# A later start for the image's split, scans moved to other steps, and one small product moved to GpSimd, in a four-layer convolution network on one core

## The chip, the cores and the metric

The kernel runs on one core of a Trainium2 chip. A core has TensorE (PE, matrix products), VectorE (DVE), ScalarE (ACT), GpSimd (POOL) and SyncE (SP), which issues most transfers. Each engine works through its own list of instructions in the order in which the program gave them, and waits on semaphores for the others. The metric is device time in microseconds (us), taken as the median of several executions. A separate execution is recorded by the hardware profiler; single durations and waits come from it.

## What is computed

The input `x` has 4 images of 32 x 32 pixels with 16 channels. Four layers follow each other, each `x = x + layer(group_norm(x))`. Layers 0, 1 and 3 are convolutions with a filter for every pixel:

```
first   = einsum('ijyx,byxc->bijc', M, inputs)
shifted = conv(inputs, kern)        # 32*32*16 filters of 3x3x16, one set for each (i, j)
diff    = relu(inputs[:, None, None] - shifted)
second  = einsum('ijyx,bijyxc->bijc', W, diff)
return first - second
```

(The last layer sums over the other pair of pixel indices.) Layer 2 is an interval layer: running maxima and minima over a 32 x 32 triangle, then two steps that take `max_k sigmoid(f[i,k] Wf + r[k,j] Wr + b)` over k, then a sigmoid of a product.

## The kernel before

Numbers of layers in the kernel count the three convolutions as 0, 1 and 2; the interval layer is done ahead of the third one, so "layer 2" in the code is the last convolution with the interval layer before it. The images go in two groups of two. A phase is one convolution layer on one group; there are six phases, in the order (group 0, layer 0), (group 1, layer 0), (group 0, layer 1), and so on. While TensorE does one phase, what the next phase needs is prepared behind it.

A phase has 8 chunks of 128 output pixels (`t`), and a chunk 32 steps: 16 channels `f` times 2 images `b`. So a phase has 256 steps, and the kernel 1536. In a step, TensorE fills one of four pairs of accumulation banks (`pc`) with 14 matmuls that run two at a time: `first_part` does those with WU and WL, then ScalarE scales the pair (L607), then `second_part` does those with WD and W9. Then VectorE reads the pair, takes the smaller of it and zero, multiplies by the weights WT of the chunk and sums up (L623, called junk<-pc). `first_part` of a step is issued before `second_part` of the step before it. At each 32nd step VectorE also adds the sums to X (L637).

float32 values are split into a high part (their upper bits, a bit mask, L176) and the rest[...]. L176 is used on the weights (`upper_w`) and on the image (`upper_x`). "Masking" here is L176, not `mask2`, which is a small constant of the interval layer.

Three streams of other work are laid between the steps, in an order written out by generators. No scheduler moves anything.

- `prep_parts` prepares the weights, one unit (4 channels) in eight steps, two units ahead. The eight parts are: L176 on DVE; W9 on ACT (L152); WD's first half on ACT (L209), and W (L222) and two WL (L224) on POOL; WD's second half, and `prep` of the next unit on POOL (L186); WU (L212) on ACT with WD (L213) on POOL, twice; the load of a later unit's weights on SP (L101); nothing. Each part ends with a `yield` that says whether the step is free for other work ("idle"): true for the first and the last two, false for the rest.
- `behind(phase)` does everything else for the next phase: in layer 2 `interval_layer`, then `before_conv`, then the first terms. What it yields is the number of steps until it is asked again; `IDLE` (0) means the next step that the weights' stream calls idle.
- `conv_layer` runs the steps and asks both.

`before_conv` normalizes the image, writes it to DRAM (L340) and reads it back as shifted copies, 24 transfers into `raw` (L350, on SP). After a last `yield 4`, `split` makes the image's parts for each of the two images: L176 on DVE, iz on POOL (L253), iy on ACT (L257), im on ACT (L152) and later on DVE (L155), iyz on POOL (L260). With layers 0 and 1, and when the second group is prepared, the first-term matmuls (L380) come after it, with their transposes and sums (L387, L390).

`interval_layer` transposes (L463), fills (L471), runs two scans of 512 elements in each direction (`running`, L481), a reordering copy between the directions on POOL (L488) and a triangle select (L492). Then `right_side` (L515, copies L518), `left` (L502, copy L527), and `step` twice, with names a and b: eight sums of 33 x 33 on POOL (L534), each followed six steps later by a maximum on DVE (L541), then a sigmoid (L545) and four transfers (L547). `constants` makes the layer's constants early in phase 0; `mask2` is reduced on DVE (L405), and half of it is negated on DVE (L409).

In the trace a wait of DVE for `raw<-xs` is a wait for the shifted copies.

Of the kernel before, what the change touches and what calls it, by code (L numbers as in the profile page):

```python
# [19 lines left out]
GC = GB * C  # L20
# [21 lines left out]
def net_kernel(ctx: ExitStack, tc: tile.TileContext, x, xq, xi, convs, iv_w, iv_b, out):  # L42
# [21 lines left out]
    nc = tc.nc  # L64
# [23 lines left out]


    IDLE = 0  # L90
    RAWS = 2
    PLAIN = 2
    AHEAD = 2
    FIRST = 3
    raws, units, chunks = {}, {}, {}

    def load_raw(u):
        if u < n_chunks * NU:
            n = u // NU
            raws[u] = wpool.tile([P, 4, FU, P], F32, tag="raw", bufs=RAWS, name=f"raw_{u}")  # L100
            nc.sync.dma_start(raws[u], convs[phases[n // NT][1]][2][n % NT, u % NU])  # L101
# [49 lines left out]
    def halve(dst, src, mask):  # L151
        nc.scalar.activation(dst, src, AF.Copy, scale=mask[:, 1:2])  # L152
# [16 lines left out]
    def image(v, x):  # L169
        return v.rearrange("... (y x) -> ... y x", x=x)[..., :H]  # L170

    def upper(src, name):

        t = work.tile([P, 2, NH], F32, tag="upper", bufs=2, name=f"upper_{name}")
        t = t.rearrange("p s (y x) -> p s y x", x=src.shape[3])
        nc.vector.tensor_scalar(  # L176
            t.bitcast(I32), src.bitcast(I32), HIGH, None, op0=ALU.bitwise_and
        )
        return t.rearrange("p s y x -> p s (y x)")
# [12 lines left out]
    def prep_parts():  # L192

        for u in range(PLAIN, n_chunks * NU):
            units[u] = [
                wpool.tile([P, 2, FU, P], F32R, tag=tag, bufs=AHEAD + 1, name=f"{tag}_{u}")
                for tag in ("WU", "WL", "WD")  # L200
            ] + [wpool.tile([P, FU, P], F32R, tag="W9", bufs=AHEAD + 1, name=f"W9_{u}")]
            src = raws.pop(u)
            w8 = src[:, :2].rearrange("p s f k -> p s (f k)")
            w9 = src[:, 2]
            WU, WL, WD = (t.rearrange("p s f k -> p s (f k)") for t in units[u][:3])
            W9 = units[u][3]

            def scaled(s):
                nc.scalar.activation(WD[:, s], high[:, s], AF.Copy, scale=-EPS)  # L209

            def difference(s):
                nc.scalar.copy(WU[:, s], high[:, s])  # L212
                nc.gpsimd.tensor_tensor(  # L213
                    WD[:, s], WD.bitcast(F32)[:, s], WL.bitcast(F32)[:, s], ALU.add
                )

            high = upper(src[:, :2], f"w{u}")
            yield True
            halve(W9, w9, low_w)
            yield False  # L220
            scaled(0)
            nc.gpsimd.tensor_tensor(W9, W9.bitcast(F32), src[:, 3], ALU.add)  # L222
            for s in range(2):
                nc.gpsimd.tensor_tensor(WL[:, s], w8[:, s], high[:, s], ALU.subtract)  # L224
            yield False
            scaled(1)
            prep(u + 1)
            yield False
            difference(0)
            yield False  # L230
            difference(1)
            yield False
            load_raw(u + RAWS)
            yield True
            yield True

    def prep_plain(u, at=0, to=FU, eng=nc.gpsimd):
        if at == 0:
# [8 lines left out]

    def split(eng, g, b, name, pause=IDLE):

# [24 lines left out]
    def group_norm(g, name, dst, gap):  # L274
# [40 lines left out]
        yield 2  # L315
        yield IDLE
        rstd = work.tile([P, GC // 2], F32, tag="rstd", name=f"rstd_{name}")
# [10 lines left out]
    def before_conv(g, layer):  # L328
        xn = work.tile([P, NT, GC], F32, tag="xn", bufs=2, name=f"xn_{g}_{layer}")
        xns[g] = xn  # L330
        yield from group_norm(g, f"c{g}{layer}", xn, 1 if layer == 2 else 4)

        nc.vector.transpose(  # L335
            xt[g][:, :, 1 : 1 + H], xn
        )
        inner = xs[g][:, HP : HP + H * HP].rearrange("p (t r n) -> p r t n", r=ROWS, n=HP)
        for r in range(ROWS):
            nc.sync.dma_start(inner[:, r], xt[g][GC * r : GC * (r + 1)])  # L340
        yield 2
        xsv = xs[g].rearrange("(b c) n -> c b n", b=GB)
        at = 0
        for slot, row, tap in [(2, row, 8) for row in range(4)] + [
            (tap // 4, tap % 4, tap) for tap in range(8)
        ]:
            for h in range(2):
                off = (HI * h + tap // 3) * HP + tap % 3
                r0 = 64 * h + C * row
                nc.sync.dma_start(  # L350
                    raw[r0 : r0 + C, slot, :, :RUN], xsv[:, :, off : off + RUN]
                )
            at += 1
            if at % 3 == 0:
                yield 1
        yield 4
        for b in range(GB):
            yield from split(nc.gpsimd, g, b, f"{g}{layer}")
            yield IDLE
            halve(image(im9[g][:, b], H), image(raw[:, 2, b], HP), low_x)  # L360
            for s in range(2):
                difference(nc.gpsimd, g, b, s)
            yield 3
            halve_rest(image(im9[g][:, b], H), image(raw[:, 2, b], HP), low_x)
            yield 1
# [35 lines left out]
    def constants():  # L401
        nc.scalar.dma_start(wv, iv_w)
        nc.scalar.dma_start(bv, iv_b)
        mask2 = const.tile([P, GB], F32, name="mask2")
        nc.vector.tensor_reduce(  # L405
            mask2, ident.rearrange("p (s b c) -> p b s c", b=GB, c=C), axis=AX.XY, op=ALU.add
        )

        nc.vector.tensor_scalar_mul(mask2[GC : 2 * GC], mask2[GC : 2 * GC], -1.0)  # L409
        yield 2  # L410

        def blocks(dst, k, mask, n, p0=0):
            p = dst.shape[0]
            nc.gpsimd.tensor_tensor(
                dst,
                wv[p0 : p0 + p, k, :].unsqueeze(1).to_broadcast([p, n, C]),
                mask[p0 : p0 + p].unsqueeze(2).to_broadcast([p, n, C]),
                ALU.mult,
            )

        nc.gpsimd.memset(rt, 0.0)
        yield 1


        for k, hidden, name in ((0, None, "f0"), (3, 2, "f1"), (6, 5, "f2")):
            n = 64 if hidden is None else 96
            t = const.tile([n, GB, C], F32, name=name)
            blocks(t[:64], k, mask2, GB)
            if hidden is not None:
                blocks(t[64:], hidden, mask2, GB, 64)  # L430
            iv[name] = t.rearrange("p k c -> p (k c)")
            yield 1
        for k, name in ((1, "r0"), (4, "r1")):
            t = const.tile([64, NQ * GB, C], F32, name=name)
            for q in range(NQ):
                blocks(t[:, q * GB : (q + 1) * GB, :], k, mask2, GB)
            iv[name] = t.rearrange("p k c -> p (k c)")
            yield 1
    def interval_layer(g):
# [4 lines left out]
        n = H * H  # L444
# [19 lines left out]
        yield 2  # L464
        yield IDLE
        nc.scalar.mul(one[GC:], one[:GC], -1.0)
# [10 lines left out]
        def running(dst, src):  # L477

            for half in range(2):
                o = slice(n // 2 * half, n // 2 * (half + 1))  # L480
                nc.vector.tensor_tensor_scan(  # L481
                    dst[:, o], resets[:, o], src[:, o], 0.0, op0=ALU.add, op1=ALU.max
                )
                yield 3


        yield from running(one[:, ::-1], other[:, ::-1])
# [36 lines left out]
        def step(name, ftp, bias):  # L524
# [6 lines left out]
            for i in range(QI + 1):  # L531
# [11 lines left out]
                yield 6  # L543
            yield IDLE
            nc.scalar.activation(s, s, AF.Sigmoid, bias=bias)  # L545
# [98 lines left out]
    def conv_layer(phase, behind):  # L644


        wait, when_idle = 0, False
        accs[phase] = work.tile([P, NT, GC], F32, tag="acc", bufs=2, name=f"acc_{phase}")
        for t in range(NT):
            n = phase * NT + t  # L650
            steps = [(f, b) for f in range(C) for b in range(GB)]
            if n == 0:
                steps.sort(key=lambda s: (s[0] // FU, s[1]))
            for at, (f, b) in enumerate(steps):
                idle = next(parts, True) if n or at >= FIRST else True
                if at == 4:
                    load_chunk(n + 1)
                step = (phase, t, f, b)
                open_steps.append((step, first_part(step)))
                if len(open_steps) > 1:  # L660
                    second_part(*open_steps.pop(0))
                wait -= 1
                if wait <= 0 and (idle or not when_idle):
                    wait = next(behind, 1 << 20)
                    when_idle = wait == IDLE
        for _ in behind:
            pass

# [167 lines left out]
    parts = prep_parts()  # L836
    for phase in range(len(phases)):
        conv_layer(phase, behind(phase))
# [78 lines left out]
```

## Time and profile before

| | |
|---|---|
| median of 3 executions | 2600.67 us (2600.32 to 2601.96) |
| the profiled execution | 2597.44 us, recorded span 2595.7 us |
| mean granted TensorE clock | 0.999 |
| L623, DVE, x1536 | 1878.9 us, 1223 ns each |
| L607, ACT, x1520 | 1531.5 us, 1008 ns each |
| L176 on weights, DVE, x190 | 140.2 us, 738 ns each |
| L481 scan, DVE, x8 | 11.9 us, 1491 ns each |
| L409, DVE, x1 | 3.8 us |
| L541 maxima, DVE, x32 | 41.0 us, 1281 ns each |
| L534 sums, POOL, x32 | 75.8 us, 2367 ns each |
| transfers raw<-xs, x120 | 67.8 KB each, 2.4 us to landing |

How to read it: the page gives the busy time of each engine. The list of waits says which engine stood idle for which other, in total, how often, and the longest. The timeline gives single instructions: start, duration, engine, line, operation, output and inputs, and in brackets the idle time just before and what ended it. The table of windows gives the busy time of each engine in a stretch, and the granted TensorE clock in its column PEclk (1.00 is full speed). A duration on DVE or POOL includes time in which the instruction was already issued and could not go on.

### The profile page before, as it was taken

How to read it: one execution, taken by the hardware profiler on the slowest of the kernel's cores; microseconds unless marked ns; L12 is line 12 of the kernel's file. 1: busy time of each engine (PE TensorE's matmuls, PEld its weight loads, DVE VectorE, ACT ScalarE, POOL GpSimd, SP SyncE). 2: the span in 40 equal slices, each digit the busy share in tenths (PEclk: the TensorE clock that was granted, in tenths of full speed). 3: DMA queues.
4: the chain of work that ended last, by engine and by line, in shares of the span. 5: the costliest groups of instructions: out<-in, count | busy, mean ns of one | idle time of the engine just before them, and what ended most of it. 6: DMA issues, size and time to landing. Idle time of an engine off the chain costs nothing.

```text
span 2595.7 us, 56475 instructions
## 1 busy us (share of the span) xinstructions
PE 2561.7 (99%) x21906; PEld 2048.5 (79%) x21906; DVE 2151.6 (83%) x3652; ACT 2094.7 (81%) x2549; POOL 1564.6 (60%) x1288
## 2 busy tenths in 40 slices
PE   8999999999999999999999999999999999999999
PEld 5887888878888877888887877787777777788887
DVE  8887778888777877777888988889889888777777
ACT  4787888888888877888887888888888888788886
POOL 4656555575555556555566766576767666455553
PEclk9999999999999999999999999999999999999999
DMA  4423222232222432222222222322222234222220
GB/s 152 165 79 114 90 90 92 83 129 88 87 95 90 153 117 76 97 90 90 91 98 90 90 84 86 123 93 90 78 89 97 92 118 155 76 99 90 90 91 19
DMA packets 50285, 254.14 MB, mean 98 GB/s; under 512 B 12129, under 2 KB 14049, under 8 KB 24929
## 3 DMA queue, kind: packets, MB, share of 16 engines
q1 hardware_dynamic: 49056, 249.94, 28.3%
q8 instruction: 172, 2.82, 0.4%
q14 instruction: 97, 0.79, 0.1%
q10 hardware_dynamic: 832, 0.58, 0.1%
q0 software_dynamic: 128, 0.02, 0.0%
HBM read 248.99 MB, written 0.98 MB: 96 GB/s over the span
## 4 chain that ended last, share of the span: by engine, by line
PE 92%; DVE 3%; DMA 2%; issue 2%; SPq 1%; ACT 1%; DVEq 0%; ACTq 0%
PE pc L577 91%; DVE junk L623 2%; SPq L350 1%; PE pf L380 1%; DMA raw<-in_g 1%; DMA raw<-xs 1%; ACT pc L607 0%; DMA xs<-xt 0%; SPq L340 0%; DVE upper_w L176 0%; PE ps_l L502 0%; DMA XQ<-in_xq 0%; DVE s_b L541 0%; PE ps_r L515 0%; DVE xt L335 0%
## 5 line engine op out<-in xcount | busy, mean ns | idle before, releaser
L623 DVE SCALAR_TENSOR_TENSOR junk<-pc,WT 128x1024 f32<-128x1024 f32 x1536 | 1878.9, 1223 | 399.8 <-PE pc L577 355.4
L607 ACT ACTIVATE pc<-pc 128x1024 f32<-128x1024 f32 x1520 | 1531.5, 1008 | 446.9 <-PE pc L577 385.6
L577 PE MATMUL pc<-iy,WU 64*128 64x512 f32 x6080 | 968.7, 394 | 18.5 <-DVE junk L623 18.5
L577 PE MATMUL pc<-iyz,WD 64*128 64x512 f32 x6080 | 965.6, 393 | 3.3 <-ACT pc L607 2.6
L577 PE MATMUL pc<-iz,WL 64*128 64x512 f32 x6080 | 964.3, 393 | 0.0
L222 POOL TENSOR_TENSOR W<-W,raw 128x512 fp32r<-128x512 f32 x190 | 250.7, 1320 | 832.1 <-ACT W L152 829.0
L577 PEld LDWEIGHTS pc<-iy,WU 64*128 64x128 f32 x6080 | 577.0, 185 | 162.4 <-DVE junk L623 27.2
L577 PEld LDWEIGHTS pc<-iyz,WD 64*128 64x128 f32 x6080 | 579.0, 185 | 141.2 <-ACT pc L607 6.6
L577 PEld LDWEIGHTS pc<-iz,WL 64*128 64x128 f32 x6080 | 580.1, 185 | 133.6
L577 PE MATMUL pc<-im,W 64*128 64x512 f32 x3072 | 621.4, 397 | 0.0
L224 POOL TENSOR_TENSOR WL<-raw,upper_w 128x512 fp32r<-128x512 f32 x380 | 487.3, 1305 | 4.4 <-DVE upper_w L176 4.4
L213 POOL TENSOR_TENSOR WD<-WD,WL 128x512 fp32r<-128x512 f32 x380 | 488.5, 1308 | 0.0
L577 PEld LDWEIGHTS pc<-im,W 64*128 64x128 f32 x3072 | 293.4, 185 | 71.1 <-issue 3.6
L209 ACT ACTIVATE WD<-upper_w 128x512 fp32r<-128x512 f32 x380 | 237.1, 624 | 10.9 <-DVE upper_w L176 10.9
L212 ACT CAST WU<-upper_w 128x512 fp32r<-128x512 f32 x380 | 233.5, 615 | 1.3 <-issue 1.3
L186 POOL TENSOR_TENSOR raw<-raw,pick 128x512 f32<-128x512 f32 x190 | 201.2, 1059 | 7.9 <-DMA raw<-in_g 5.3
L176 DVE TENSOR_SCALAR upper_w<-raw 128x1024 int32<-128x1024 int32 x190 | 140.2, 738 | 0.1
L152 ACT ACTIVATE W<-raw,low_w 128x512 fp32r<-128x512 f32 x190 | 135.9, 715 | 0.1
L623 DVE DVE_READ_ACCUMULATOR junk<-pc,WT 128x1 f32 x1536 | 127.3, 83 | 0.0
L534 POOL TENSOR_TENSOR tables<-ft_b,rt 128x1089 f32<-128x1089 f32 x16 | 37.9, 2366 | 5.3 <-ACT ft_b L527 5.3
L534 POOL TENSOR_TENSOR tables<-ft_a,rt 128x1089 f32<-128x1089 f32 x16 | 37.9, 2368 | 0.0
L253 POOL TENSOR_TENSOR iz<-raw,upper_x 128x512 fp32r<-128x512 f32 x20 | 23.8, 1202 | 23.2 <-DVE upper_x L176 23.2
(134 smaller groups left out, 384.2 us busy)
## 6 DMA issues: line engine op xcount, KB each, us to landing
raw<-in_g SPq DMA_DIRECT2D x190, 1024.0 KB, 4.9
WT<-in_w SPq DMA_DIRECT2D x48, 512.0 KB, 3.5
MT<-in_mt SPq DMA_DIRECT2D x6, 2048.0 KB, 12.2
raw<-xs SPq DMA_DIRECT2D x120, 67.8 KB, 2.4
raw<-in_xi SPq DMA_DIRECT2D x3, 271.0 KB, 4.8
raw<-in_xi SPq DMA_DIRECT2D x1, 813.0 KB, 8.1
first<-in_g SPq DMA_DIRECT2D x1, 768.0 KB, 8.6
xs<-xt SPq DMA_DIRECT2D x20, 34.0 KB, 2.1
```

The lines of the kernel that those rows point to most:

```text
L152: nc.scalar.activation(dst, src, AF.Copy, scale=mask[:, 1:2])
L176: nc.vector.tensor_scalar(t.bitcast(I32), src.bitcast(I32), HIGH, None, op0=ALU.bitwise_and)
L186: eng.tensor_tensor(raws[u][:, 1, at:to], raws[u][:, 1, at:to], pick[:, f0 + at : f0 + to].unsqueeze(2).to_broadcast([P, to - at, P]), ALU ...
L209: nc.scalar.activation(WD[:, s], high[:, s], AF.Copy, scale=-EPS)
L212: nc.scalar.copy(WU[:, s], high[:, s])
L213: nc.gpsimd.tensor_tensor(WD[:, s], WD.bitcast(F32)[:, s], WL.bitcast(F32)[:, s], ALU.add)
L222: nc.gpsimd.tensor_tensor(W9, W9.bitcast(F32), src[:, 3], ALU.add)
L224: nc.gpsimd.tensor_tensor(WL[:, s], w8[:, s], high[:, s], ALU.subtract)
L534: nc.gpsimd.tensor_tensor(t, ft[:, i, :].unsqueeze(1).to_broadcast([P, T1, T1]), rt, ALU.add,)
L577: nc.tensor.matmul(ps[:, h, :], lhsT=w[r], rhs=v[r], start=first and k == 0, stop=k == len(pairs) - 1, skip_group_check=not first,)
L607: nc.scalar.activation(ps, ps, AF.Copy, scale=1.0 + EPS)
L623: nc.vector.scalar_tensor_tensor(junk, ps.rearrange("p h n -> p (h n)"), 0.0, chunks[n], op0=ALU.min, op1=ALU.mult, accum_out=accs[phase][ ...
```

## The change

Three things are changed. `before_conv` yields 12 steps (7 in layer 2) in place of 4 between the last transfers of the shifted copies and `split`. In `running`, each scan waits for a step that the weights' stream calls CALM, a new second kind of step: the third, fourth and fifth of its eight parts; after a scan the yield is 1 in place of 3. `conv_layer` is rewritten to know the two kinds; a positive yield and IDLE mean what they meant. The negation in `constants` goes from VectorE to GpSimd.

```diff
+    CALM = -1
...
             high = upper(src[:, :2], f"w{u}")
-            yield True
+            yield (IDLE,)
             halve(W9, w9, low_w)
-            yield False
+            yield ()
             scaled(0)
...
-            yield False
+            yield (CALM,)
             scaled(1)
             prep(u + 1)
-            yield False
+            yield (CALM,)
             difference(0)
-            yield False
+            yield (CALM,)
             difference(1)
-            yield False
+            yield ()
             load_raw(u + RAWS)
-            yield True
-            yield True
+            yield (IDLE,)
+            yield (IDLE,)
...
-        yield 4
+        yield 7 if layer == 2 else 12
         for b in range(GB):
             yield from split(nc.gpsimd, g, b, f"{g}{layer}")
...
-        nc.vector.tensor_scalar_mul(mask2[GC : 2 * GC], mask2[GC : 2 * GC], -1.0)
+        nc.gpsimd.tensor_scalar_mul(mask2[GC : 2 * GC], mask2[GC : 2 * GC], -1.0)
...
                 o = slice(n // 2 * half, n // 2 * (half + 1))
+                yield CALM
                 nc.vector.tensor_tensor_scan(
                     dst[:, o], resets[:, o], src[:, o], 0.0, op0=ALU.add, op1=ALU.max
                 )
-                yield 3
+                yield 1
...
-        wait, when_idle = 0, False
+        kind, wait = 1, 0
...
-                idle = next(parts, True) if n or at >= FIRST else True
+                may = next(parts, (IDLE, CALM)) if n or at >= FIRST else (IDLE, CALM)
...
                 wait -= 1
-                if wait <= 0 and (idle or not when_idle):
-                    wait = next(behind, 1 << 20)
-                    when_idle = wait == IDLE
+                if wait <= 0 and (kind > 0 or kind in may):
+                    kind = wait = next(behind, 1 << 20)
```

## The prediction

> **What bounds the kernel now.** Time is set by TensorE (page, parts 1 and 4):
>
> ```profile
> PE 2561.7 (99%) x21906; PEld 2048.5 (79%) x21906; DVE 2151.6 (83%) x3652; ACT 2094.7 (81%) x2549; POOL 1564.6 (60%) x1288
> ...
> PE 92%; DVE 3%; DMA 2%; issue 2%; SPq 1%; ACT 1%; DVEq 0%; ACTq 0%
> ```
>
> No matmul is changed, so only TensorE's idle time can be won or enlarged. The wait views of PE and of DVE:
>
> ```profile
> PE pc L577 <- DVE junk L623: 18.5, 14, 3.0
> ...
> PE pc L577 <- ACT pc L607: 2.6, 6, 0.6
> ```
>
> ```profile
> DVE junk L623 <- PE pc L577: 355.4, 937, 1.2
> DVE upper_x L176 <- DMA raw<-xs: 19.3, 5, 4.7
> ```
>
> DVE idles 355 us yet holds TensorE up 14 times: bursts. Asking for the PE waits window by window places all 14. Five stalls (2.83, 1.31, 3.01, 2.50, 2.27; sum 11.9) follow the five L176 that wait for the shifted copies. Four (0.84 and 1.48, in each of two interval layers; 4.6) follow the scans. One (0.80) follows L409, and four (0.36, 0.20, 0.33, 0.23; 1.1) lie among step b's maxima.
>
> Rule of the burst: in DVE's timeline L623 starts every 1.63 us when it waits for matmuls and every 1.37 when behind, so DVE catches up 0.27 a step. At 210.44 L623 starts 4.7 late (due 1.63 after 204.09) and TensorE stalls 2.83; so about 2.0 us of lateness are free (four PSUM pairs), and the rest is a stall.
>
> A stall costs more than its gap. The third one in PE's timeline, and the clock after it:
>
> ```profile
> 957.60 1.22 PE L577 MATMUL pc<-iy,WU 64*128 64x512 f32 x4 [3.01 <-DVE junk L623]
> ...
> 960.69 0.63 PE L577 MATMUL pc<-iy,WU 64*128 64x512 f32 x4
> ```
>
> ```profile
> 957.20:960.60 3.40, 3.00 (x14) 2.41 (x16) 3.27 (x7) 2.82 (x4) 3.02 (x3) 0.50 0.19 80
> ```
>
> Seven matmul pairs take 3.09 us where a full-speed step takes 1.63: the clock column says 0.50. The 2.83 stall is followed by the same (213.1 to 216.5); the 2.50 one is not. I price the two half-clock stretches at 3.09 - 1.63, about 1.5 us each. And any stall has 0.26 of restart: at the fourth one the im matmuls start at 1683.09 and, a step later, at 1687.49; 4.40 less the usual 1.63 is 2.76, for a gap of 2.50.
>
> [...]L409 on 32x2 elements ends at 114.21, just when GpSimd's row ends at 114.19; scans take 1.21 beside an idle GpSimd and 1.70 to 1.85 beside L213. [...]here 2.83 and 3.01 cost the clock, 2.50 didn't.
>
> **The change, part by part.**
>
> *Longer wait (yield 4 to 12, to 7 in layer 2).* Counting L623 in the instruction orders of both kernels, L176 on the image moves from steps 112, 304, 560 to 120, 312, 568, and from 992, 1248 to 995, 1251. SP's order is unchanged, so the copies land when they did: 4.5, 3.0, 4.7, 4.0, 3.2 us after DVE came for them. DVE now comes 8 x 1.63 = 13 or 3 x 1.63 = 4.9 us later, so all five are there, with 0.9 us to spare in the fourth, and being under 2.0 late would be free. Removed: 11.9 + 5 x 0.26 + 2 x 1.5 = 16.2. Moved along: iz, iyz on POOL, iy, im on ScalarE, L155, and in layers 0 and 1 the first-term matmuls with L387 and L390. None of these issues a DMA. Eight steps keep the place relative to the weights' preparation (period 8), and where they stood they made DVE at most 1.5 late (L623 at 241.18, its matmuls done at 239.66): under 2.0, so nothing. In layer 2 the first L176 on the image comes one read after a mask and may find POOL at W or WL: 0.1 + 0.1 + 1.3 late at most, free too; the last L155 stays at 1014, ten steps before it is needed. Bounds: gain 16.2; if the two layer-2 transfers are later still by 2 us, 11.
>
> *L409 to GpSimd.* It leaves DVE's queue, where L623 stood behind 3.81 us:
>
> ```profile
> 110.40 3.81 DVE L409 TENSOR_SCALAR mask<-mask 32x2 f32<-32x2 f32 x1
> ```
>
> On POOL it stands between the two L213 of one unit; the nearest row, L306 TENSOR_SCALAR on POOL, is 254 ns. Behind it wait WD and the small L414, and the unit's matmuls come eight steps later: hidden. Removed: 0.80 + 0.26 = 1.1. The 0.72 stall just before comes from ScalarE's late L607 behind the issue of L403 and stays. Bounds 0 to 1.3.
>
> *Scans.* Before (DVE, then POOL):
>
> ```profile
> 1365.55 1.85 DVE L481 TENSOR_TENSOR_SCAN tables<-tables 64x512 f32<-64x512 f32 x1
> ...
> 1373.43 1.68 DVE L176 TENSOR_SCALAR upper_w<-raw 128x1024 int32<-128x1024 int32 x1
> ...
> 1387.11 1.21 DVE L481 TENSOR_TENSOR_SCAN tables<-tables 64x512 f32<-64x512 f32 x1
> 1388.24 1.71 DVE L176 TENSOR_SCALAR upper_w<-raw 128x1024 int32<-128x1024 int32 x1
> ```
>
> ```profile
> 1365.00 3.49 POOL L213 TENSOR_TENSOR WD<-WD,WL 128x512 fp32r<-128x512 f32 x2
> 1372.45 2.10 POOL L488 COPY tables<-tables 64x1024 f32<-64x1024 f32 x1 [3.95 <-DVE tables L481]
> ```
>
> Line 1373.43 is a mask behind L488, which the second scan released; lines 1387.11 and 1388.24 are scan and mask on end. The four scans now precede L623 number 807, 813, 821, 823 (were 806, 809, 815, 818); masks stay at 802, 810, 818, 826. So at least three reads (L623) lie between a scan and the next mask, but all four stand where POOL works. A scan delays L623 by 0.93 alone (1370.02 to 1372.31, less 1.37) and 1.57 locked (1364.40 to 1367.33). By the 0.27 rule lateness goes: 0.3 before 807, about 1.5 after; 0.8 before 813, 1.1 to 2.0 after; under 0.5 before 821, 0.8 to 1.1 after; 0.55 to 0.85 at 822, and the scan at 823 probably stands behind L213: 2.3. That is a stall of 0.3 + 0.26 per layer, 1.1 in both. Removed: 2 x (0.84 + 1.48 + 2 x 0.26) = 5.7. Net 4.6; bounds 0 (every scan waits out a whole L213 of 1.3) and 5.7.
>
> *What moves with them.* L488, L492, the right-side matmuls L515 with their copies L518, L502, L527 and L534 go along by one to five steps; PE does the same matmuls, and L492 (1.26 on POOL) has five steps before L515 needs it. Step a's maxima L541 move from 837 ... 879 to 840 ... 882. L545 with its four DMAs on SP waits for an idle slot and stays, and so does step b at 904 ... 946. Modulo 32, step a now lies exactly as step b does, and step b is where the last four stalls are. At a multiple of 32, L637 comes just ahead of a maximum:
>
> ```profile
> 1572.35 1.50 DVE L637 SCALAR_TENSOR_TENSOR X<-acc,X 128x32 f32<-128x32 f32 x1
> 1573.77 1.28 DVE L541 TENSOR_REDUCE s_b<-tables 128x33 f32<-128x1089 f32 x1
> ```
>
> L637 waits there for L534 on POOL (1571.42 to 1573.80), and POOL's order around it is the same in both steps now. So step a takes over step b's cost: 0.36 + 0.20 + 2 x 0.26 = 1.1 per layer. Added: 2.2; bounds 0 and 3.
>
> *Sum.* 16.2 + 1.1 + 4.6 - 2.2 = 19.7 us against the profiled span of 2595.7. That execution took 2597.44, so it lies 3.2 below the median; the stalls are fixed by the program, so I subtract from the median: 2600.67 - 19.7 = 2581.0.
>
> **Rivals.** (1) The scans win nothing, as the lock meets each of them, and step a pays: 16.2 + 1.1 - 2.2 = 15.1, or 2585.6; with step a at 3 each and the tight layer-2 waits half paid, 2588. For it: POOL is busy at all four places. Against: no mask follows close. (2) Step a doesn't inherit the stalls and the scans are free: 23.0, or 2577.7. Against: equal orders. (3) The copies aren't what it says: the landing moves along with the wait, and only scans and mask gain: 3.5, or 2597.2. Against: SP issues the copies back to back for 11 us whatever DVE does. (4) Slower: POOL becomes the bound between the scans and the end of step a (806 to 882, ten units of 8 steps in each interval layer). Each lock holds POOL up, WD comes late, and TensorE waits for it. A unit lasts 8 x 1.63 = 13.1 us; POOL's work in it is 7.4 (L222, two L224, L186, two L213) and 8/6 of an L534 of 2.37: 10.6. The room is 2.5 us a unit, and weights are ready some six steps, 10 us, ahead, another 1.0 over ten units. So it decides from 3.5 us of lock a unit, and eats up the gains from 4.5 (19.7 over twenty units is 1.0). At 5 us: 2 x (10 x 2.5 - 10) = 30, or 2611. Against: the locked unit seen here lost 1.0 (L213 3.49 for 2.54), and PE waited for POOL 0.7 us in all.
>
> **How the numbers follow.** Forecast 0.64 (2578 to 2584), (1) 0.22, (2) 0.07, (3) 0.04, (4) 0.03. Measurement tells about 0.2%, 5.2 us, from no change: faster means under 2595.5. Forecast, (1) and (2) are all faster, and so is a part of the range between (1) and (3): 0.94; same 0.035; slower 0.025. Range 2577.5 to 2588: it takes in (2) and (1).
>
> **What would show it.** Right: no DVE wait for raw<-xs (before 19.3 us), no clock of 0.50 between start and end; L409 gone from DVE, about 0.25 us on POOL; PE's wait for L623 down from 18.5 to 3 or 4 us; new stalls near 1465 in step a; at most small ones at the scans. Wrong: waits for raw<-xs left in layer 2, stalls over 1 us at the fourth scan, or PE waiting for WD.

## The result, and the profile after

The changed kernel takes 2578.74 us (median of 4 executions, 2578.01 to 2578.97); the kernel before, beside it, 2600.49 (2597.4 to 2601.96). The ratio is 0.9917, with a 95% interval of 0.9900 to 0.9935: 21.7 us less, faster by 0.8%. The profiled spans are 2576.3 and 2595.7 us, 19.4 apart. In the line numbers of the changed kernel, L176 has become L177, L409 L410, L481 L483, L534 L536, L541 L543, L577 L579, L607 L609, L623 L625 and L637 L639.

The page of the changed kernel, parts 1 and 4:

```profile
PE 2558.4 (99%) x21906; PEld 2058.9 (80%) x21906; DVE 2150.0 (83%) x3651; ACT 2094.3 (81%) x2549; POOL 1565.7 (61%) x1289
...
PE 97%; DVE 2%; issue 1%; ACT 0%; DMA 0%; DVEq 0%; ACTq 0%
```

PE's share of the chain of waits has gone from 92% to 97%, and the transfers (2%) have left it. Its waits, and those of DVE:

```profile
PE pc L579 <- ACT pc L609: 3.0, 7, 0.6
PE pc L579 <- DVE junk L625: 2.3, 8, 0.4
```

```profile
DVE junk L625 <- PE pc L579: 351.3, 928, 1.2
...
DVE junk L625 <- DMA raw<-xs: 0.2, 1, 0.2
```

TensorE's wait for the reading of the sums is down from 18.5 us to 2.3. What is left is eight stalls of about 0.36 and 0.20, four of them in the two steps a and four in the two steps b. None of the five masks of the image waits for the shifted copies any more, where DVE waited 19.3 us before: the 0.2 us left under that name stand before an L625, not before a mask.

The first mask of the image, in DVE's timeline, now follows its L625 at once, where it stood 4.50 us before:

```profile
214.90 1.22 DVE L625 SCALAR_TENSOR_TENSOR junk<-pc,WT 128x1024 f32<-128x1024 f32 x1 [0.40 <-PE pc L579]
216.05 0.69 DVE L177 TENSOR_SCALAR upper_x<-raw 128x1024 int32<-128x1024 int32 x1
216.66 1.22 DVE L625 SCALAR_TENSOR_TENSOR junk<-pc,WT 128x1024 f32<-128x1024 f32 x1
```

Two of the scans, and the mask after them:

```profile
1364.46 2.03 DVE L483 TENSOR_TENSOR_SCAN tables<-tables 64x512 f32<-64x512 f32 x1
...
1381.18 2.02 DVE L483 TENSOR_TENSOR_SCAN tables<-tables 64x512 f32<-64x512 f32 x1
...
1386.97 0.69 DVE L177 TENSOR_SCALAR upper_w<-raw 128x1024 int32<-128x1024 int32 x1
```

The scans have become longer (1.72, 2.03, 1.30 and 2.02 us in this layer; 1.85, 1.21, 1.70 and 1.21 before), since they stand where GpSimd works. This longer time beside the other engine is what "lock" stands for in the prediction and in one expectation below: in the kernel before a scan took 1.21 beside an idle GpSimd and 1.85 beside L213 (at 1365.55), and the two L213 took 3.49 there where two took 2.54 elsewhere (at 1379.71). How the two engines hold each other up was not shown. But the mask after them is 0.69 long and three L625 away, and between 1340 and 1400 us the list names no wait of PE.

The negation on GpSimd:

```profile
111.24 0.22 POOL L410 TENSOR_SCALAR mask<-mask 32x2 f32<-32x2 f32 x1
```

3.81 us on DVE have become 0.22 on GpSimd. And step a, in DVE's timeline, where the kernel before had no stall:

```profile
1450.40 1.51 DVE L639 SCALAR_TENSOR_TENSOR X<-acc,X 128x32 f32<-128x32 f32 x1
1451.83 1.28 DVE L543 TENSOR_REDUCE s_a<-tables 128x33 f32<-128x1089 f32 x1
...
1455.53 1.31 DVE L177 TENSOR_SCALAR upper_w<-raw 128x1024 int32<-128x1024 int32 x1
```

It is the picture of step b from the prediction, almost to the hundredth: L639 held for 1.51, a maximum right behind it, then a mask held for 1.31.

### The profile page after: what moved, and what is told of

It is laid out like the page before. It is cut to its first block, busy times and chain, and to the rows that moved or that the text cites. A ratio compares the mean times of both kernels' runs of the same rounds, so it can differ in the third digit from the quotient of the medians.

```text
span 2576.3 us, 56475 instructions
## 1 busy us (share of the span) xinstructions
PE 2558.4 (99%) x21906; PEld 2058.9 (80%) x21906; DVE 2150.0 (83%) x3651; ACT 2094.3 (81%) x2549; POOL 1565.7 (61%) x1289
## 4 chain that ended last, share of the span: by engine, by line
PE 97%; DVE 2%; issue 1%; ACT 0%; DMA 0%; DVEq 0%; ACTq 0%
PE pc L579 96%; DVE junk L625 1%; PE pf L381 1%; ACT pc L609 0%; PE ps_l L504 0%; DMA XQ<-in_xq 0%; DVE s_a L543 0%; DVE s_b L543 0%; PE ps_r L517 0%; DVE X L639 0%; ACT L547 0%; ACT L319 0%; ACT s_a L547 0%; PE ps_y L565 0%; DVE raw L786 0%
## 5 line engine op out<-in xcount | busy, mean ns | idle before, releaser
L625 DVE SCALAR_TENSOR_TENSOR junk<-pc,WT 128x1024 f32<-128x1024 f32 x1536 | 1879.2, 1223 | 401.3 <-PE pc L579 351.3
L609 ACT ACTIVATE pc<-pc 128x1024 f32<-128x1024 f32 x1520 | 1531.6, 1008 | 445.6 <-PE pc L579 383.9
L579 PE MATMUL pc<-iy,WU 64*128 64x512 f32 x6080 | 967.5, 394 | 2.7 <-DVE junk L625 2.3
L579 PE MATMUL pc<-iyz,WD 64*128 64x512 f32 x6080 | 965.6, 393 | 3.0 <-ACT pc L609 3.0
L579 PE MATMUL pc<-iz,WL 64*128 64x512 f32 x6080 | 964.0, 392 | 0.0
L579 PEld LDWEIGHTS pc<-iy,WU 64*128 64x128 f32 x6080 | 579.7, 185 | 141.6 <-DVE junk L625 9.9
L579 PEld LDWEIGHTS pc<-iyz,WD 64*128 64x128 f32 x6080 | 580.9, 185 | 138.5 <-ACT pc L609 8.6
L579 PEld LDWEIGHTS pc<-iz,WL 64*128 64x128 f32 x6080 | 582.4, 185 | 129.7
L579 PE MATMUL pc<-im,W 64*128 64x512 f32 x3072 | 621.8, 397 | 0.0
L214 POOL TENSOR_TENSOR WD<-WD,WL 128x512 fp32r<-128x512 f32 x380 | 488.4, 1309 | 0.1
L579 PEld LDWEIGHTS pc<-im,W 64*128 64x128 f32 x3072 | 294.5, 185 | 69.2 <-issue 3.4
L213 ACT CAST WU<-upper_w 128x512 fp32r<-128x512 f32 x380 | 233.7, 615 | 0.9 <-issue 0.9
L177 DVE TENSOR_SCALAR upper_w<-raw 128x1024 int32<-128x1024 int32 x190 | 136.6, 719 | 0.1
L625 DVE DVE_READ_ACCUMULATOR junk<-pc,WT 128x1 f32 x1536 | 127.7, 83 | 0.0
L536 POOL TENSOR_TENSOR tables<-ft_b,rt 128x1089 f32<-128x1089 f32 x16 | 38.0, 2373 | 5.3 <-ACT ft_b L529 5.3
L536 POOL TENSOR_TENSOR tables<-ft_a,rt 128x1089 f32<-128x1089 f32 x16 | 37.9, 2366 | 4.6 <-ACT ft_a L529 4.6
```

The source lines that it names most:

```text
L177: nc.vector.tensor_scalar(t.bitcast(I32), src.bitcast(I32), HIGH, None, op0=ALU.bitwise_and)
L214: nc.gpsimd.tensor_tensor(WD[:, s], WD.bitcast(F32)[:, s], WL.bitcast(F32)[:, s], ALU.add)
L536: nc.gpsimd.tensor_tensor(t, ft[:, i, :].unsqueeze(1).to_broadcast([P, T1, T1]), rt, ALU.add,)
L579: nc.tensor.matmul(ps[:, h, :], lhsT=w[r], rhs=v[r], start=first and k == 0, stop=k == len(pairs) - 1, skip_group_check=not first,)
L609: nc.scalar.activation(ps, ps, AF.Copy, scale=1.0 + EPS)
L625: nc.vector.scalar_tensor_tensor(junk, ps.rearrange("p h n -> p (h n)"), 0.0, chunks[n], op0=ALU.min, op1=ALU.mult, accum_out=accs[phase][ ...
```

## The experiments

**One part alone.** Three kernels are the kernel before with one part of the change each. The longer wait:

```diff
-        yield 4
+        yield 7 if layer == 2 else 12
```

> The kernel before with the longer wait alone (12 steps, 7 in layer 2). If the shifted copies' late landing is what cost the time: all five DVE waits for raw<-xs (19.3 us) gone, PE's wait for L623 down from 18.5 to about 6.6, no half-clock stretch; 15 to 16 us less in the profiled span (five stalls 11.9, five restarts of 0.26, two half-clock stretches of 1.5), and up to 18 less in the median, if the median execution of the kernel before has one more half-clock stretch than the profiled one had. If instead the scans' place is what mattered: under 5 us.

Measured: 2582.35 us (2581.03 to 2583.84), ratio 0.9926 (0.9913 to 0.9938), about 19 us less in the median; the profiled span is 2581.3, 14.4 less, a little under the expected 15 to 16. Its waits of PE and of DVE:

```profile
PE pc L577 <- DVE junk L623: 7.9, 10, 1.8
```

```profile
DVE upper_x L176 <- DMA raw<-xs: 1.6, 1, 1.6
```

Four of the five waits for the copies are gone, and there is no half-clock stretch before the kernel's end. In the fifth SP took 15.5 us from the first to the last issue of this group, 13.7 before; DVE waited 1.6 and TensorE stalled 0.4. So the wait carries most of the gain, and the 7 steps of layer 2 have little room: over the profiles with this wait the last copy of a layer-2 group lands up to 1.4 us before DVE comes for it, or up to 1.6 after. PE's wait came out at 7.9 instead of 6.6 mainly because L409's stall was 1.80 here, without ScalarE's stall ahead of it.

The two kinds of steps and the scans alone (the change without the longer wait and with L409 on VectorE):

> The kernel before with the two kinds of steps and the scans' new places alone. If scans stall TensorE only where a mask follows close: stalls of 0.84 and 1.48 at the scans gone in both interval layers (4.5 to 5.7 us), but 0.36 and 0.20 new in each step a (2.2 us with restarts): 2 to 3.5 us less in all. If the lock with GpSimd is what counts, wherever the scan stands: no gain from the scans and 2 us slower.

Measured: 2598.53 us, ratio 0.9993 (0.9985 to 1.0002): in time alone not to be told from no change. In its profile all four stalls at the scans are gone and four of 0.36 and 0.20 stand in the two steps a, as in the changed kernel. The gain of the scans and its price are both there; the difference, some 2 us, is smaller than what the times of the kernel before vary by.

L409 alone:

```diff
-        nc.vector.tensor_scalar_mul(mask2[GC : 2 * GC], mask2[GC : 2 * GC], -1.0)
+        nc.gpsimd.tensor_scalar_mul(mask2[GC : 2 * GC], mask2[GC : 2 * GC], -1.0)
```

> The kernel before with L409 on GpSimd alone. If L409's 3.81 us on DVE is what stalls TensorE at 114 us: the 0.80 stall there gone, 1.1 to 1.4 us less; the interval is as wide as that, so the profile decides. If it was ScalarE's late L607 all along: both stalls stay, no gain.

Measured: 2598.69 us, ratio 0.9986 (0.9979 to 0.9993): 3.6 us less, from 1.8 to 5.5. Between 100 and 130 us its PE waits for ScalarE alone:

```profile
PE pc L577 <- ACT pc L607: 0.4, 1, 0.4
```

L409's stall is gone, ScalarE's stays. The gain is larger than forecast; the next runs show what can add to it.

**The kernel before, profiled twice more**, unchanged.

> The kernel before, profiled again. If the clock is halved by chance after stalls of 2 to 3 us: the number of half-clock stretches differs from the two of the first profile, each adding about 1.5 us to the span of 2595.7, while the gaps stay 18.5 in all. If it depends on the length of the stall alone: two stretches again, after the first and third DVE wait.

> The kernel before, profiled once more. If chance decides: another number of half-clock stretches, or other stalls that they follow. If the length of the stall alone decides: two, after the first and third DVE wait.

Measured: 2601.14 us with a span of 2599.4, and 2602.76 with 2601.1. PE's waits for L623 are 19.6 us in both (18.5 in the first profile). The half clock came in periods of 3.4 us, two in the first profile, four in the one and six in the other here. The windows of the second (the two that follow each other are one stretch of 6.8 us), with the granted clock in the third column from the right:

```profile
115.90:119.30 3.40, 3.40 (x20) 2.66 (x18) 3.11 (x7) 2.10 (x3) 1.58 (x2) 0.50 1.02 434
535.80:539.20 3.40, 3.40 (x20) 2.69 (x18) 3.27 (x6) 2.67 (x4) 3.02 (x3) 0.50 0.01 2
959.00:962.40 3.40, 3.40 (x20) 2.68 (x18) 2.93 (x5) 2.36 (x4) 3.14 (x3) 0.50 0.02 5
1686.10:1689.50 3.40, 2.68 (x12) 2.17 (x14) 3.27 (x6) 2.82 (x5) 3.03 (x3) 0.50 0.67 277
1689.50:1692.90 3.40, 3.40 (x18) 2.66 (x16) 1.61 (x4) 1.90 (x3) 3.40 (x4) 0.50 0.00 0
2123.00:2126.40 3.40, 3.40 (x20) 2.65 (x18) 3.27 (x6) 2.06 (x3) 3.03 (x4) 0.50 0.35 140
```

The first of them follows L409, in PE's timeline of the same run:

```profile
114.72 0.73 PE L577 MATMUL pc<-iy,WU 64*128 64x512 f32 x4 [1.81 <-DVE junk L623]
```

So the clock was lost after a stall of 1.81 us. In the kernel with the scans alone it was kept after one of 3.01:

```profile
1684.64 0.73 PE L579 MATMUL pc<-iy,WU 64*128 64x512 f32 x4 [3.01 <-DVE junk L625]
```

```profile
1683.30:1686.70 3.40, 2.06 (x18) 1.69 (x20) 3.27 (x7) 3.22 (x5) 2.80 (x3) 1.00 0.88 361
```

Two, four and six periods in three profiles of one program, whose stalls for L623 add up to nearly the same (18.5, 19.6 and 19.6 us). What a period costs can be read from the extra time of the steps around a stall (the spacing of a step's im matmuls to the next step's, less 1.63 us), less the stall and its 0.26: 1.3 to 1.6 us, and 2.6 for the two in a row. How many of the stalls are paid for twice differs from one execution to the next.

**How much wait is enough.** The changed kernel with 6 and with 5 steps in every layer.

```diff
-        yield 7 if layer == 2 else 12
+        yield 6
```

> The changed kernel with a wait of 6 steps in every layer (12, and 7 in layer 2). DVE comes two steps (3.3 us) later than in the kernel before, where it waited 4.5, 3.0, 4.7, 4.0 and 3.2 us. If about 2 us of DVE's lateness are free: waits of raw<-xs of about 1.2, 0, 1.4, 0.7, 0 us and no stall at them, the changed kernel's time within 1 us (2577 to 2579). If each us of wait costs a us: about 3 us more.

> The same with 5 steps: DVE comes 1.6 us later than in the kernel before. If about 2 us are free: waits of 2.9, 1.4, 3.1, 2.4, 1.6 us, of which 1.2, 0, 1.4, 0.7, 0 come through as stalls, with restarts 3 to 5 us more than the changed kernel, and hardly a half-clock stretch[...]. If each us of wait costs a us: 10 us more or above.

Measured: 2581.68 us (2581.04 to 2583.34) with 6 steps and 2586.41 (2584.01 to 2589.91) with 5: 2.9 and 7.7 us more than the changed kernel above. Neither expectation held in full. The two kernels' waits of PE, and then of DVE; 6 steps:

```profile
PE pc L579 <- DVE junk L625: 5.0, 12, 0.8
```

```profile
DVE upper_x L177 <- DMA raw<-xs: 5.8, 4, 1.8
```

5 steps:

```profile
PE pc L579 <- DVE junk L625: 9.1, 13, 1.7
```

```profile
DVE upper_x L177 <- DMA raw<-xs: 14.0, 5, 3.4
```

There is a free part: with 5 steps DVE waits 14.0 us and TensorE stalls 1.36, 0.72, 1.74, 1.40 and 0.94 behind it, 6.2 in all. That leaves (14.0 - 6.2) / 5, about 1.6 us a wait: 1.7 in four of them and 1.2 in the fifth. I had 2.0, but that is all the lateness that L623 may have, and the mask of the image itself takes up about 0.4 of it (0.69 less the 0.27 that DVE catches up in a step). With 6 steps the mask also stands right before a mask of the weights, as the first one in DVE's timeline shows, and waits of up to 1.8 came through as stalls of 0.59, 0.71, 0.48 and 0.22:

```profile
208.43 0.69 DVE L177 TENSOR_SCALAR upper_x<-raw 128x1024 int32<-128x1024 int32 x1 [1.67 <-DMA raw<-xs]
209.03 0.69 DVE L177 TENSOR_SCALAR upper_w<-raw 128x1024 int32<-128x1024 int32 x1
```

So the 2.9 us more with 6 steps are near the 3 us of the second expectation, but not because each us of wait costs a us: the waits were 5.8 us, the stalls behind them 2.0. Both profiles also hold a stall of 0.83 in the second interval layer that the changed kernel's doesn't have: with 6 steps a mask of the weights right behind a maximum took 1.81 us there, and 0.68 in the changed kernel. In the profile these 1.1 us come on top (with the restart), so its span is 5.3 us longer. No half-clock stretch is in either profile before the end; the longest stall behind L625 there is 1.74 us.

**The stalls that the change moved into step a.** First, the maxima of both steps three steps later, away from L639 (on the changed kernel):

```diff
             nc.scalar.copy(ft, ftp)
-            yield 2
+            yield 5
...
                 last = t
-                yield 6
+                yield 6 if i < QI else 3
```

> The changed kernel, with the maxima of both steps a and b three steps later (and the last pause of the loop three shorter), so that none comes right behind L637. If the eight stalls of 0.36 and 0.20 come from L637, held by GpSimd's L534, just ahead of a maximum and a mask: all eight gone, 4 x 1.09 = 4.4 us less than the changed kernel, about 2574.4. If the maxima stall by their number and length: no change, 2578.7.

Measured: 2577.38 us (2574.48 to 2580.81). Two of the four groups of stalls are gone (step a of the first layer, step b of the second); in the two others they became larger. One of these, in DVE's timeline and in POOL's:

```profile
1557.71 3.33 DVE L639 SCALAR_TENSOR_TENSOR X<-acc,X 128x32 f32<-128x32 f32 x1
```

```profile
1556.13 2.56 POOL L214 TENSOR_TENSOR WD<-WD,WL 128x512 fp32r<-128x512 f32 x2
1558.62 2.37 POOL L536 TENSOR_TENSOR tables<-ft_b,rt 128x1089 f32<-128x1089 f32 x1
```

L639 came in the middle of L214, and waited not for its end at 1558.7 but through the L536 that followed it without a gap: 3.33 us, for an instruction of 0.19. In step a of the first layer the same L639 got in between the two (1.03 us). So neither rival fits: the maxima do not stall by themselves, yet moving them does not help either. It is L639's wait. How long that is, when GpSimd has two instructions back to back, does not follow from when L639 comes: in the four places it came 0.28 to 0.33 us into an L214, and waited 1.03 and 1.06 in two, 3.33 and 3.39 in the others.

Then the sum into X taken off DVE (on the changed kernel):

```diff
-            nc.vector.scalar_tensor_tensor(
-                X[g][:, t], acc, 1.0 / EPS, X[g][:, t], op0=ALU.mult, op1=ALU.add
-            )
+            if t < NT - 1:
+                nc.gpsimd.tensor_scalar_mul(acc, acc, 1.0 / EPS)
+                nc.gpsimd.tensor_tensor(X[g][:, t], X[g][:, t], acc, ALU.add)
+            else:
+                nc.vector.scalar_tensor_tensor(
+                    X[g][:, t], acc, 1.0 / EPS, X[g][:, t], op0=ALU.mult, op1=ALU.add
+                )
```

> The changed kernel, with the sum into X (L639) as two instructions on GpSimd (a product, then a sum) instead of one on VectorE, for all chunks but the last of each phase. If the stalls of steps a and b come from L639 waiting on VectorE for GpSimd's row to end: all eight (0.36 and 0.20) gone, 4.4 us less than the changed kernel. GpSimd gets about 0.5 us more in every 52; if that matters, PE waits for WD appear. If the maxima stall by themselves: no gain.

> The changed kernel again, beside the others on one chip. If the half-clock stretches make the spread of the kernel before, this one, which has no stall above 0.6 us, spreads by about 1 us around 2578.7. If the chips differ: a wider spread, or another median.

Measured: 2574.00 us (2573.36 to 2574.55), and the changed kernel beside it 2577.49 (2577.27 to 2578.13): 3.5 us less, with spans of 2572.4 and 2576.4. In the list of PE's waits DVE's L625 no longer stands; only ScalarE and the kernel's start are left:

```profile
PE ps_own L749 <- DVE s L747: 4.5, 1, 4.5
PE pc L579 <- ACT pc L609: 3.3, 7, 0.8
PE pc L579 <- DVE raw L790: 1.8, 1, 1.8
PE ps_v L741 <- DVE by_batch_v L740: 1.5, 1, 1.5
```

POOL's timeline shows where the two instructions have gone, ahead of L536 in time that GpSimd had:

```profile
1450.74 0.29 POOL L640 TENSOR_SCALAR acc<-acc 128x32 f32<-128x32 f32 x1 [0.91 <-DVE junk L625]
1451.11 0.25 POOL L641 TENSOR_TENSOR X<-X,acc 128x32 f32<-128x32 f32 x1
1451.32 2.37 POOL L536 TENSOR_TENSOR tables<-ft_a,rt 128x1089 f32<-128x1089 f32 x1
```

All eight stalls are gone, and this kernel is the fastest of all that ran. Of the 4.4 us expected, 0.5 went back to ScalarE's stall at step 56, which the two profiles show at 1.04 and 0.58 of extra time. And the changed kernel, run again, spreads by 0.9 us; the kernel before spread by 10 in the 8 executions beside it (2594.63 to 2604.71).

## Why the prediction was right

The sum was 19.7 us against the profiled span; the spans differ by 19.4. By its terms, read from the extra time of the steps:

| term | predicted | profiled pair |
|---|---|---|
| longer wait: stalls, restarts, two half-clock stretches | 16.2 less | 16.1 less, and 1.4 more at steps 124, 316, 572, 1004, 1013 and 1260: 14.8 |
| L409 | 1.1 less | 1.4 less |
| scans | 5.7 less, 1.1 left: 4.6 | 4.6 less |
| step a | 2.2 more | 2.2 more |
| start of the kernel | nothing | 0.8 less |

The causes were right: each of the three parts, run alone, removed the stalls that it was said to remove. That the sums lie within 0.3 us is partly luck. The start is chance: the extra time of the first 50 steps lies between 7.2 and 8.3 us over all profiles, whatever the kernel. It hides part of the 1.4 us behind the longer wait, which the prediction did not have. GpSimd did not become the bound (rival 4): the changed kernel's list names no wait of PE for it.

- *The longer wait* did what it says. All five groups of copies had landed when DVE came. For the fourth the room was as forecast: by the trace's record of landings the last copy was there at 1670.4, and the mask started at 1671.3. The 1.4 is new: behind all five masks ScalarE's L609 comes late by 0.1 to 0.2 once or twice, because iy and W, or in layer 2 im and W, now fall into the same step on ScalarE. The prediction had followed the lateness of DVE there, not that of ScalarE.
- *L409*: the mechanism was right, the term too small. In the first profile the stall of 0.72 hid a part of L409's. (The list of waits there names GpSimd's L213 for it, which ended together with ScalarE's L607; with L409 moved it names ScalarE.) The two together were worth 1.5 there; in the second repeat ScalarE was in time and L409's stall was 1.81 by itself. The 0.72 that was to stay came out at 0.40. The half clock may follow too, as it did in the second repeat; that this makes up the 3.6 us (1.8 to 5.5) of L409 alone in the median is inferred.
- *Scans*: the lateness worked out for L623 was 1.5, 1.1 to 2.0, 0.8 to 1.1 and 2.3 after the four scans; the trace has 1.47, 1.96, 0.97 and 2.13. The stall of 0.3 came out at about 0.1, with 0.26 of restart. A cost was left out: the right-side matmuls that moved along ("PE does the same matmuls") and the left one behind them take 2.3 us of extra time in their new place and took 2.0 before, in each layer and in the kernel with the scans alone too. The two errors offset each other, so the net of 4.6 is in part luck. The rival that the scans win nothing is refuted by the kernel with the scans alone: the scans do take longer where GpSimd works (up to 2.03 us in the changed kernel, 1.21 beside an idle GpSimd), but a scan has three reads to recover before the next mask.
- *Step a* took over step b's stalls: 0.64 + 0.47 and 0.63 + 0.47 of extra time. The cause named, L639 waiting for GpSimd, is shown by taking it off DVE.
- *What L409 waited for* was read too simply. L409 ended with "GpSimd's row", but that row was more than one instruction. It came at 110.40 and ended at 114.21, and POOL's timeline of the kernel before shows what it waited through:

```profile
110.72 2.52 POOL L213 TENSOR_TENSOR WD<-WD,WL 128x512 fp32r<-128x512 f32 x2
113.17 1.02 POOL L421 MEMSET rt<- 128x1089 f32 x1
```

- *From span to median* a step failed: "the stalls are fixed by the program, so I subtract from the median". The gaps nearly are, but not the half-clock periods. The first profile has two, the repeats four and six, so the median execution holds more than the profiled one. The changed kernel has none to lose, so the median fell by 21.7 where the profiled span fell by 19.4. The record has the mean granted clock of every execution, and it agrees. Of 50 of the kernel before, 7 had 0.999 and took 2597.9 us in the mean, 13 had 0.998 (2599.3), 19 had 0.997 (2602.9), 8 had 0.996 (2604.5) and 3 had 0.995 (2606.7). All 9 of the changed kernel had 0.999 or 1.000. A period at half clock lowers the mean by about 0.0007 (half of 3.41 in 2600), so 2.2 us for 0.001 is about 1.5 us a period, an estimate that fits the price above.
- *The clock* was read wrongly in one point: "2.83 and 3.01 cost the clock, 2.50 didn't" suggested that length decides. A stall of 3.01 kept the clock and one of 1.81 lost it. The starts of the half-clock periods say more: in the second repeat the first three are at 115.9, 535.8 and 959.0, apart by 123.0 and 124.0 times 3.413, which is the length in us of both periods in the first profile.

## What to carry to other kernels

Where one engine is busy all the time, ask of each helper engine not how busy it is but how late it can get before the buffers are used up, and follow its lateness step by step past each change: that gave the lateness behind the four scans to within 0.2 us, two of them as ranges. A step that is moved takes its neighbours with it: look for a place in the same trace that already has the new neighbours, and read the price there. And profile the kernel before more than once when its times spread: a stall whose cost differs from one execution to the next (two, four and six half-clock periods in three profiles here) is worth more than one profile shows.

## What the runs showed of the hardware

- The half-clock periods lay on a common spacing. In the first profile of the kernel before, both lasted 3.41 us (213.09 to 216.50 and 957.19 to 960.60), and their starts were 744.1 apart, 218 times 3.413. In the second repeat the starts at 115.9, 535.8, 959.0, 1686.1 and 2123.0 were 123, 124, 213 and 128 times 3.413 apart.
- In six stalls, where the stall fell on this spacing went with the loss of the clock, and its length did not. The stall of 3.01 in the kernel with the scans alone lasted from 1681.63 to 1684.64; 1683.32, which is 127 times 3.413 ahead of the half clock at 2116.8, cut it into 1.69 and 1.32: kept. The stall of 1.81 in the second repeat, from 112.91 to 114.72, lay whole in the stretch from 112.52 to 115.93, where the half clock began: lost. In the first profile the stalls of 2.83 and 3.01 had 2.05 and 2.60 us in the stretch ahead of the half clock: lost. Those of 2.50 and 2.27, cut in the same way, had at most 1.76 and 1.68 in one stretch: kept. Six stalls are few for a rule, and what the clock goes by was not shown.
- The clock did not always come back after one period. In the second repeat TensorE stood idle for 0.72 us of the half-clock period at 1686.1, and a second one followed; with 0.40 in the first profile (at 957.2) and 0.54 in the first repeat (at 2120.2) none did. Three cases are few for a rule. A period cost 1.3 to 1.6 us, the two in a row 2.6.
- An instruction of VectorE that came while GpSimd worked did not always end with GpSimd's running one: in the kernel with the maxima moved L639, 0.19 in the median, took 1.03 and 1.06 us in two places, and 3.33 and 3.39 in two others, through two instructions that stood back to back. L409 took 3.81 in the kernel before, through two L213 and a MEMSET.
- A stall of TensorE behind DVE cost 0.26 to 0.27 us beyond its gap, for short and long ones: stalls of 0.36 (changed kernel), 2.50 (kernel before) and 3.01 (scans alone) that kept the clock made 0.63, 2.77 and 3.28 of extra time.
